# Layer 0 of a two-layer net: feature parts stored once and repeated by the loads, and other places for three streams in a step

## The chip, the cores and the metric

The kernel runs on one core of one Trainium2 chip. Its time is the device time of one execution in microseconds, median over runs.

## What is computed

64 batches of 128 rows of 128 features go through two layers, each of an attention and a mixture of experts, each added to its input through a tanh gate. The change touches the attention of layer 0, a cross-attention whose scores are taken on exponential features:

```python
def _feature_map(x, fm_w, fm_b):
    z = jnp.einsum('nshd,ed->nshe', x, fm_w) + fm_b
    return jnp.concatenate([jnp.exp(z), jnp.exp(-z)], axis=-1)

v, k, q = (_feature_map(x, fm_w, fm_b) for x in (v, k, q))     # 16 heads of 8 -> 16 features
scores = jnp.einsum('nqhd,nkhd->nhqk', q, k) / jnp.sqrt(128.)
attn = jax.nn.softmax(scores, axis=-1)
out = jnp.einsum('nhql,nlhd->nqhd', attn, v)
...
x = x + jnp.tanh(g_xattn[0]) * (out @ fc_w.T + fc_b)           # q from layernorm(x), k and v from the context (77 rows)
x = x + jnp.tanh(g_ffn[0]) * ffn0(layernorm(x))                # 8 experts, 1 to 6 of them by a router
x = x + jnp.tanh(g_xattn[1]) * attention1(layernorm(x), context)   # relative positions
x = x + jnp.tanh(g_ffn[1]) * ffn1(layernorm(x))                # 8 experts, two per row
```

## The kernel before

**Units and steps.** In layer 0 the 64 batches make 16 groups of four for the experts and 32 units of two for the attention (NU = 2; UT = 256 columns of queries, UK = 154 of context). Step k works on several units at once, each in another stage, as Python generators ("streams"): `l0_project(k-3)`, `l0_weighted(k-2)`, `l0_maxima(k-1)` and `l0_features(k)`; in every second step the router of a group; and beside them the `tape` of the experts, some 16 parts in a step. Two steps are a pair: an even step with the router, an odd one without. Layer 1 has its own steps after these.

**What sets the order.** `weave` calls the streams' parts by time within the step. `PLAN` gives each stream (start, end, priority, behind): its parts are spread evenly between the shares start and end of a step; the priority is handed to the scheduler, which orders the instructions of each engine; `behind` = n makes the PE instructions of the stream stand after the (n+1)th last part of the experts traced so far. Each engine then takes its instructions in this order. All DMAs of layer 0 go out on SP's queue (`nc.sync`), in order.

**The attention of a unit, in four streams.**

- `l0_features` (L290): loads x and the context, layer norm, transposes (pt, L304 and L306), one matmul (pz, L311), four exps on ACT into f, the values' transposes (pv, L327). As f32 products are taken from bf16 parts, `split3` (L132) cuts f into three bf16 parts f3: cast on DVE, subtract on POOL, cast, subtract. The product of two such numbers takes six pairs of parts, and these six stand as 96 rows (6 pairs × 16 features of a head) of qst for the queries and kst for the context. To get from 128 partitions (features × heads) to these rows, the parts go through DRAM: `stack_out` stores dq and dk with each part repeated as the pairs want it (six stores, L144 and L146, 1,230 KB), and four loads (L340, L342) bring 48 rows at a time to qst and kst, in rows of 512 and 308 bytes.
- `l0_maxima` (L346): scores S (L355) of all heads, maxima mx over the context (L358), a transpose pn (L363), and the negated maxima in three bf16 parts, n3 (L366 to L369), sent as three rows of 8 KB into qst, rows 96 to 98 (L371). kst has ones there, so that the second product takes the maximum away by itself.
- `l0_weighted` (L373): ST (L396), the scores again, transposed and without their maxima; exp to P (L399); products with the values, AV (L385), which also give the denominators; a copy to av (L388) and a store to od in DRAM (L408, 512 KB). Then `normalize` (L428): denominators den from od (L435), o in two loads (L439), a reciprocal on DVE (L440), dr to DRAM sixteen times repeated (L442, 256 KB), rr back (L445), o times rr on POOL (L446).
- `l0_project` (L411): the output product pf (L420) and x1.

The experts (`l0_ffn`) make three-fold f32 products on PE by a helper (L165 to L167) with the tiles pg, pu and py; between them ACT and DVE compute t (L516 to L518), ACT hh (L523) and POOL hl (L524).

Of the kernel before, what the change touches and what calls it, by code (L numbers as in the profile page):

```python
# [10 lines left out]
F32 = mybir.dt.float32  # L11
F32R = mybir.dt.float32r
BF16 = mybir.dt.bfloat16
AF = mybir.ActivationFunctionType
# [6 lines left out]
KL = 77  # L21
NH = 16
# [6 lines left out]
NU = 2  # L29
UT = NU * S  # L30
UK = NU * KL
# [10 lines left out]
def weave(tc, streams, marks=None):  # L42
# [27 lines left out]
PARTS0, PARTS1 = 33, 24  # L70

PLAN = dict(
    out=(0,0.2,2000,0),
    wei=(0, 0.7, 0, 6),
    max=(0.05, 0.8, 1000, None),
    fea=(0.2, 0.6, 500, None),
    out1=(0.1, 0.25, 600, None),
    att1=(0.25, 1.1, 0, 8),
    rel1=(0.32, 0.88, 0, 3),
# [25 lines left out]
class Net:  # L105
# [26 lines left out]
    def split3(self, f, out3):  # L132
# [3 lines left out]
        nc.gpsimd.tensor_tensor(f, f, out3[:, 0], ALU.subtract)  # L136
        nc.vector.tensor_copy(out3[:, 1], f)
        nc.gpsimd.tensor_tensor(out3[:, 2], f, out3[:, 1], ALU.subtract)  # L138

    def stack_out(self, dq, dk, f3, nq):  # L140

        nc = self.nc
        for n, c, p in ((0, 3, 0), (3, 2, 1), (5, 1, 2)):
            nc.sync.dma_start(out=dq[n : n + c].rearrange("i p t -> p i t"),  # L144
                              in_=f3[:, p, :nq].unsqueeze(1).to_broadcast([128, c, nq]))
            nc.sync.dma_start(out=dk[n : n + c].rearrange("i p t -> p i t"), in_=f3[:, :c, nq:])  # L146

    def stack_q(self, dq, f3, nq):
        for n, c, p in ((0, 3, 0), (3, 2, 1), (5, 1, 2)):
# [140 lines left out]
    def l0_features(self, u, st):  # L290
        nc, i, tc = self.nc, self.i, self.tc
        a, pm, dp = self.ap, self.pmisc, self.dp
        b0 = u * NU
        kst, (vf, va) = self.kst[u % 3], self.va[u % 3]
        xg = self.f0.tile([128, NU, 128], F32, tag="xg", bufs=4, name="xg")
        nc.sync.dma_start(out=xg, in_=i["x"][b0 : b0 + NU].rearrange("b p d -> p b d"))
        cg = a.tile([KL, NU, 128], F32, tag="cg", bufs=2, name="cg")
        nc.sync.dma_start(out=cg, in_=i["ctx_1024"][b0 : b0 + NU].rearrange("b p d -> p b d"))
        xn = self.layernorm(xg, NU, a, "a")
        nc.gpsimd.tensor_tensor(xg, xg, self.fcb.unsqueeze(1).to_broadcast([128, NU, 128]), ALU.add)  # L300
        NT = UT + UK
        pt = pm.tile([128, 512], F32, tag="misc", name="pt")
        for b in range(NU):
            nc.tensor.transpose(pt[:, b * S : (b + 1) * S], xn[:, b, :], self.ident)  # L304
        for b in range(NU):
            nc.tensor.transpose(pt[:, UT + b * KL : UT + (b + 1) * KL], cg[:, b, :], self.ident[:KL, :KL])  # L306
        xT = a.tile([128, NT], F32, tag="xT", bufs=1, name="xT")
        nc.scalar.copy(xT, pt[:, :NT])
        yield
        pz = pm.tile([128, 512], F32, tag="misc", name="pz")  # L310
        nc.tensor.matmul(pz[:, :NT], lhsT=self.fmW, rhs=xT, start=True, stop=True)  # L311

        f = a.tile([128, 2 * NT], F32, tag="feat", bufs=1, name="feat")
        for n, sign in ((0, 1.0), (1, -1.0)):
            nc.scalar.activation(f[:, n * UT : (n + 1) * UT], pz[:, :UT], AF.Exp, bias=self.fmb[:, n : n + 1], scale=sign)
            nc.scalar.activation(f[:, 2 * UT + n * UK : 2 * UT + (n + 1) * UK], pz[:, UT:NT], AF.Exp,
                                 bias=self.fmb[:, n : n + 1], scale=sign)
        yield
        if u < 3:
            with tc.issue_after(self.ln_last.ins):  # L320
                nc.vector.memset(kst[96:99], 1.0)
            nc.gpsimd.memset(va[:, :, :, 16:17], 1.0)

        for b in range(NU):
            pv = pm.tile([128, 512], F32, tag="misc", name="pv")
            for s in range(2):
                nc.tensor.transpose(pv[:KL, s * 128 : (s + 1) * 128],  # L327
                                    f[:, 2 * UT + s * UK + b * KL : 2 * UT + s * UK + (b + 1) * KL], self.ident)
            nc.scalar.copy(va[:, b, :, 0:16],
                                  pv[:KL, :256].rearrange("p (c h) -> p h c", h=NH))  # L330
        f3 = a.tile([128, 3, 2 * NT], BF16, tag="f3", bufs=1, name="f3")
        yield
        self.split3(f, f3)
        yield
        dq = dp.tile([6, 128, 2 * UT], BF16, tag="dq", name="dq")
        dk = dp.tile([6, 128, 2 * UK], BF16, tag="dk", name="dk")
        self.stack_out(dq, dk, f3, 2 * UT)
        qst = a.tile([99, NH, UT], BF16, tag="qst", bufs=3, name="qst")
        for n in range(2):
            nc.sync.dma_start(out=qst[48 * n : 48 * n + 48],  # L340
                              in_=dq[:, :, n * UT : (n + 1) * UT].rearrange("i (e h) t -> (i e) h t", h=NH))
            self.last_dma = nc.sync.dma_start(out=kst[48 * n : 48 * n + 48],  # L342
                              in_=dk[:, :, n * UK : (n + 1) * UK].rearrange("i (e h) t -> (i e) h t", h=NH))
        st[u] = dict(xg=xg, qst=qst, kst=kst, va=vf, spare=[Spare(self.pGU, self.gub)] * 4 if u < 2 else [])

    def l0_maxima(self, s):  # L346
# [26 lines left out]
    def l0_weighted(self, s):  # L373

        nc, a = self.nc, self.ap
        ps_t, qst, kst, va = self.pST, s["qst"], s["kst"], s["va"]
        av = a.tile([128, 4, NU, 128], F32, tag="av", bufs=1, name="av")
        vp = self.avp
        banks = itertools.cycle([ps_t] + s["spare"][2:])

        def weigh(b, hg, p):
            for j in range(4):

                n = (b * NH + 4 * j + hg) * 17
                nc.tensor.matmul(vp[32 * j : 32 * j + 32, hg, :], lhsT=va[:, n : n + 32],  # L385
                                 rhs=p[:, j, :], start=True, stop=True, tile_position=(0, 32 * j))
            if hg == 3:
                nc.scalar.copy(av[:, :, b, :], vp)  # L388

        last = None  # L390
        for b in range(NU):
            for hg in range(4):
                st = next(banks).tile([128, 4, 128], F32, tag="ST", name="ST")
                for j in range(4):
                    h = 4 * j + hg
                    nc.tensor.matmul(st[:KL, j, :], lhsT=kst[:, h, b * KL : (b + 1) * KL],  # L396
                                     rhs=qst[:, h, b * S : (b + 1) * S], start=True, stop=True)
                p = a.tile([KL, 4, 128], F32, tag="P", bufs=3, name="P")
                nc.scalar.activation(p, st[:KL], AF.Exp, scale=1.0 / math.sqrt(128.0))  # L399
                if last:  # L400
                    weigh(*last)
                last = (b, hg, p)
                yield
        weigh(*last)
        yield
        T = NU * S
        od = self.dp.tile([4, 32, 4, T], F32, tag="od16", name="od")
        nc.sync.dma_start(out=od.rearrange("j r g t -> (j r) g t"), in_=av.rearrange("p g b q -> p g (b q)"))  # L408
        s["o"] = self.normalize(od, 16, NU)

    def l0_project(self, u, s, x1s):  # L411
        nc, pm = self.nc, self.pmisc
# [12 lines left out]
            x1s[u // 2] = self.x1n  # L425
        yield

    def normalize(self, od, nd, n):  # L428


        nc, a, dp = self.nc, self.ap, self.dp
        nch = nd * NH // 128
        T = n * S
        den = a.tile([NH * n, 128], F32, tag="den", bufs=1, name="den")
        nc.sync.dma_start(out=den, in_=od[:, nd].rearrange("j g (b q) -> j (g b) q", b=n))  # L435
        o = self.f0.tile([128, nch, T], F32, tag="o", bufs=2, name="o")
        ny = 4 // nch
        for y in range(ny):
            nc.sync.dma_start(out=o[y::ny], in_=od[:, :nd, y * nch : (y + 1) * nch].rearrange("j d c t -> d j (c t)"))  # L439
        nc.vector.reciprocal(den, den)  # L440
        dr = dp.tile([nd, NH * n, 128], F32, tag=f"dr{nd}_{n}", name="dr")
        nc.sync.dma_start(out=dr.rearrange("d p q -> p d q"),  # L442
                          in_=den.unsqueeze(1).to_broadcast([NH * n, nd, 128]))
        rr = a.tile([128, nch, T], F32, tag="rr", bufs=1, name="rr")
        nc.sync.dma_start(out=rr, in_=dr.rearrange("d (x c b) q -> (d x) c (b q)", c=nch, b=n))  # L445
        nc.gpsimd.tensor_tensor(o, o, rr, ALU.mult)  # L446
        return o

# [814 lines left out]
```

## Time and profile before

| | |
|---|---|
| three runs | 2716.01, 2718.08 and 2725.01 us; median 2718.08 |
| the profiled execution | 2721.63 us, its span 2719.9 us |
| mean granted TensorE clock | 0.94 |
| layer 0 | about the first 1345 us of the span |
| DMA | 282.16 MB, 468,652 packets |
| PE idle, 0 to 120 us, S L355 for kst<-dk | 20.6 us, 3 times, the longest 11.5 |
| PE idle, 120 to 1330 us, S L355 for kst<-dk | 28.0 us, 16 times |

The page gives the busy time of each engine: PE is TensorE's matmuls, PEld its loads of weights, DVE, ACT and POOL the vector, scalar and GpSimd engines, SP the engine that issues the DMAs. It cuts the span into 40 slices with the busy share in tenths, where PEclk is the clock that TensorE was granted, in tenths of full speed. The chain that ended last is followed back from the end, from each instruction to what released it. A row of the timeline has the start and length in us, the engine, the line and operation with its tiles (out<-in), and in brackets the idle time ahead of it and what ended that. "L355" is line 355 of the kernel.

### The profile page before, as it was taken

How to read it: one execution, taken by the hardware profiler on the slowest of the kernel's cores; microseconds unless marked ns; L12 is line 12 of the kernel's file. 1: busy time of each engine (PE TensorE's matmuls, PEld its weight loads, DVE VectorE, ACT ScalarE, POOL GpSimd, SP SyncE). 2: the span in 40 equal slices, each digit the busy share in tenths (PEclk: the TensorE clock that was granted, in tenths of full speed). 3: DMA queues.
4: the chain of work that ended last, by engine and by line, in shares of the span. 5: the costliest groups of instructions: out<-in, count | busy, mean ns of one | idle time of the engine just before them, and what ended most of it. 6: DMA issues, size and time to landing. Idle time of an engine off the chain costs nothing.

```text
span 2719.9 us, 60927 instructions
## 1 busy us (share of the span) xinstructions
PE 2409.3 (89%) x23574; PEld 1655.9 (61%) x23574; DVE 1996.1 (73%) x4165; ACT 1563.2 (57%) x3030; POOL 1551.5 (57%) x1508
## 2 busy tenths in 40 slices
PE   3688989999989899999897798998999998999996
PEld 2466666666666666666565565666666666666654
DVE  3368788888888888887785466776677676766676
ACT  2455555656555556555454356666666666666665
POOL 4455465555565555554566355665666666656556
PEclk9989899999999999999997689999999999999999
DMA  6744355354454443453235655545555655655400
GB/s 140 172 107 93 78 114 117 93 107 104 83 122 106 94 111 91 100 120 73 57 80 130 137 115 112 119 110 107 107 112 109 121 127 116 126 111 109 95 16 8
DMA packets 468652, 282.16 MB, mean 104 GB/s; under 512 B 231030, under 2 KB 446974, under 8 KB 468267
## 3 DMA queue, kind: packets, MB, share of 16 engines
q1 hardware_dynamic: 440715, 237.89, 43.4%
q10 hardware_dynamic: 27648, 40.38, 4.3%
q8 instruction: 185, 3.03, 0.5%
q14 instruction: 104, 0.85, 0.1%
HBM read 143.00 MB, written 134.40 MB: 102 GB/s over the span
## 4 chain that ended last, share of the span: by engine, by line
PE 49%; DMA 16%; DVE 13%; POOL 9%; issue 7%; ACT 3%; SPq 3%; POOLq 0%; ACTq 0%; DVEq 0%
DMA kst<-dk 5%; PE ST L837 4%; PE py L165 3%; PE py L166 3%; PE py L167 3%; PE AV L845 3%; DMA dk<-f 2%; PE AV L385 2%; POOL hl L1001 2%; PE S L780 2%; PE pu L165 2%; PE pg L165 2%; PE pz L165 2%; PE S L885 2%; POOL f L138 2%
## 5 line engine op out<-in xcount | busy, mean ns | idle before, releaser
L524 POOL TENSOR_TENSOR hl<-t,hh 128x512 fp32r<-128x512 f32 x336 | 441.8, 1317 | 352.3 <-ACT hh L523 348.2
L1001 POOL TENSOR_TENSOR hl<-t,hh 128x512 fp32r<-128x512 f32 x256 | 347.0, 1371 | 148.0 <-ACT hh L1000 145.3
L829 POOL TENSOR_TENSOR sc<-sc,mx 128x308 f32<-128x308 f32 x256 | 190.3, 747 | 229.4 <-DVE mx L828 94.8
L523 ACT CAST hh<-t 128x512 fp32r<-128x512 f32 x336 | 207.2, 617 | 162.5 <-PE py L167 68.8
L516 ACT ACTIVATE t<-pg 128x512 f32<-128x512 f32 x336 | 200.9, 598 | 158.3 <-PE pg L167 114.2
L517 DVE SCALAR_TENSOR_TENSOR t<-t,pg 128x512 f32<-128x512 f32 x336 | 227.7, 678 | 74.6 <-ACT t L516 74.0
L838 ACT ACTIVATE rel<-ST 77x512 f32<-77x512 f32 x256 | 157.7, 616 | 170.4 <-PE ST L837 166.7
L518 DVE TENSOR_TENSOR t<-t,pu 128x512 f32<-128x512 f32 x336 | 227.3, 677 | 15.1 <-PE pu L167 6.7
L623 DVE TENSOR_TENSOR ys<-sb,py 128x512 f32<-128x512 f32 x224 | 152.0, 679 | 79.2 <-PE py L167 78.3
L827 DVE TENSOR_TENSOR sc<-S,rq 128x308 f32<-128x308 f32 x256 | 120.2, 472 | 120.6 <-PE ST L837 50.3
L614 ACT COPY sb<-pb 128x512 f32<-128x512 f32 x256 | 150.5, 588 | 97.4 <-PE pb L609 94.2
L837 PE MATMUL ST<-ident,sc 128*128 128x128 f32 (+1 forms) x1024 | 173.9, 296 | 35.1 <-POOL sc L829 33.0
L1000 ACT CAST hh<-t 128x512 fp32r<-128x512 f32 x256 | 155.5, 622 | 83.6 <-PE py L167 75.0
L993 ACT ACTIVATE t<-pz 128x512 f32<-128x512 f32 x256 | 151.9, 600 | 69.9 <-POOL hl L1001 64.1
L399 ACT ACTIVATE P<-ST 77x512 f32<-77x512 f32 x256 | 151.0, 591 | 57.9 <-PE ST L396 55.1
L165 PE MATMUL py<-hh,wd_h 128*128 128x512 f32 x336 | 156.9, 467 | 18.5 <-ACT sb L614 11.9
L165 PE MATMUL pg<-xh,wg_h 128*128 128x512 f32 x336 | 159.9, 476 | 11.5 <-DVE t L518 10.5
L358 DVE TENSOR_REDUCE mx<-S 128x5 f32<-128x385 f32 (+1 forms) x192 | 110.4, 577 | 78.2 <-PE S L355 76.6
L837 PEld LDWEIGHTS ST<-ident,sc 128*128 128x128 f32 (+1 forms) x1024 | 126.4, 152 | 66.6 <-POOL sc L829 42.0
L165 PE MATMUL pu<-xh,wu_h 128*128 128x512 f32 x336 | 159.9, 476 | 5.0 <-DVE t L517 4.5
L166 PE MATMUL py<-hl,wd_h 128*128 128x512 f32 x336 | 148.6, 442 | 2.3 <-POOL hl L524 2.3
L995 DVE TENSOR_TENSOR t<-t 128x512 f32<-128x512 f32 x128 | 106.6, 833 | 50.9 <-ACT t L993 50.8
(247 smaller groups left out, 6627.4 us busy)
## 6 DMA issues: line engine op xcount, KB each, us to landing
rq<-ra SPq DMA_DIRECT2D x256, 154.0 KB
qst<-dq SPq DMA_DIRECT2D x96, 384.0 KB
ra<-sg ACTq DMA_DIRECT2D x128, 192.5 KB
kst<-dk SPq DMA_DIRECT2D x96, 231.0 KB
dq<-f SPq DMA_DIRECT2D x47, 384.0 KB
od<-av SPq DMA_DIRECT2D x32, 512.0 KB
ra<-sg ACTq DMA_DIRECT2D x64, 231.0 KB
dq<-f SPq DMA_DIRECT2D x47, 256.0 KB
```

The lines of the kernel that those rows point to most:

```text
L165: nc.tensor.matmul(ps, lhsT=wh, rhs=xh, start=start, stop=False)
L166: nc.tensor.matmul(ps, lhsT=wh, rhs=xl, start=False, stop=False)
L516: nc.scalar.activation(t, pg, AF.Tanh, scale=0.5)
L517: nc.vector.scalar_tensor_tensor(t, t, 1.0, pg, ALU.add, ALU.mult)
L518: nc.vector.tensor_tensor(t, t, pu, ALU.mult)
L523: nc.scalar.copy(hh, t)
L524: nc.gpsimd.tensor_tensor(hl, t, hh.bitcast(F32), ALU.subtract)
L829: nc.gpsimd.tensor_tensor(sc, sc, m.unsqueeze(2).to_broadcast([128, 4, KL]), ALU.subtract)
L837: nc.tensor.transpose(st[:r, j, :], sc.rearrange("q j k -> q (j k)")[:, j * KL : j * KL + r], self.ident)
L838: nc.scalar.activation(relg[:KL, hg, b], st[:KL].rearrange("k j (q e) -> k j q e", e=2), AF.Exp, scale=1.0 / math.sqrt(HD))
L1000: nc.scalar.copy(hh, t)
L1001: nc.gpsimd.tensor_tensor(hl, t, hh.bitcast(F32), ALU.subtract)
```

## The change

Three things change in layer 0.

First, `l0_features` writes f in another layout (positive exps of queries and context together, then the negative ones), so that two exps do instead of four, and stores each of the three parts once: d01 with parts 0 and 1, d2 with part 2 (615 KB in all). The repeats that the six pairs want are made by the loads, six in place of four, which read the same part of DRAM for several groups of rows: the same number of rows, of the same sizes, now at a pitch of 820 bytes for both. Two of the six need d2.

Second, `normalize` takes den straight from av in SBUF in place of od in DRAM, stores dr once (16 KB) and repeats it in the load of rr.

Third, in `PLAN` the shares of features, weighted sums and output change, and the weighted sums stand behind the experts' part two further back.

```diff
 PLAN = dict(
-    out=(0,0.2,2000,0),
-    wei=(0, 0.7, 0, 6),
+    out=(0, 0.3, 2000, 0),
+    wei=(0.15, 0.85, 0, 8),
     max=(0.05, 0.8, 1000, None),
-    fea=(0.2, 0.6, 500, None),
+    fea=(0.05, 0.45, 500, None),
...
-    def stack_out(self, dq, dk, f3, nq):
-
-        nc = self.nc
-        for n, c, p in ((0, 3, 0), (3, 2, 1), (5, 1, 2)):
-            nc.sync.dma_start(out=dq[n : n + c].rearrange("i p t -> p i t"),
-                              in_=f3[:, p, :nq].unsqueeze(1).to_broadcast([128, c, nq]))
-            nc.sync.dma_start(out=dk[n : n + c].rearrange("i p t -> p i t"), in_=f3[:, :c, nq:])
...
         for n, sign in ((0, 1.0), (1, -1.0)):
-            nc.scalar.activation(f[:, n * UT : (n + 1) * UT], pz[:, :UT], AF.Exp, bias=self.fmb[:, n : n + 1], scale=sign)
-            nc.scalar.activation(f[:, 2 * UT + n * UK : 2 * UT + (n + 1) * UK], pz[:, UT:NT], AF.Exp,
-                                 bias=self.fmb[:, n : n + 1], scale=sign)
+            nc.scalar.activation(f[:, n * NT : (n + 1) * NT], pz[:, :NT], AF.Exp, bias=self.fmb[:, n : n + 1], scale=sign)
...
-                                    f[:, 2 * UT + s * UK + b * KL : 2 * UT + s * UK + (b + 1) * KL], self.ident)
+                                    f[:, s * NT + UT + b * KL : s * NT + UT + (b + 1) * KL], self.ident)
...
-        dq = dp.tile([6, 128, 2 * UT], BF16, tag="dq", name="dq")
-        dk = dp.tile([6, 128, 2 * UK], BF16, tag="dk", name="dk")
-        self.stack_out(dq, dk, f3, 2 * UT)
+
+        d01 = dp.tile([2, 256, NT], BF16, tag="d01", name="d01")
+        d2 = dp.tile([1, 256, NT], BF16, tag="d2", name="d2")
+        for d, p0, p1 in ((d01, 0, 2), (d2, 2, 3)):
+            nc.sync.dma_start(out=d.rearrange("i (n p) t -> p (i n) t", n=2),
+                              in_=f3[:, p0:p1].rearrange("p i (n t) -> p (i n) t", n=2))
+
         qst = a.tile([99, NH, UT], BF16, tag="qst", bufs=3, name="qst")
-        for n in range(2):
-            nc.sync.dma_start(out=qst[48 * n : 48 * n + 48],
-                              in_=dq[:, :, n * UT : (n + 1) * UT].rearrange("i (e h) t -> (i e) h t", h=NH))
-            self.last_dma = nc.sync.dma_start(out=kst[48 * n : 48 * n + 48],
-                              in_=dk[:, :, n * UK : (n + 1) * UK].rearrange("i (e h) t -> (i e) h t", h=NH))
+        q, k = slice(0, UT), slice(UT, NT)
+        for to, row, n, src in ((qst, 0, 3, d01[:1, :, q]), (kst, 16, 2, d01[:, :, k]), (qst, 48, 2, d01[1:, :, q]),
+                                (kst, 80, 1, d01[:1, :, k]), (qst, 80, 1, d2[:, :, q]), (kst, 0, 1, d2[:, :, k])):
+            src = src.rearrange("i p t -> (i p) t")
+            rows = n * src.shape[0] // 16
+            if n > 1:
+                src = src.unsqueeze(0).to_broadcast([n, *src.shape])
+            self.last_dma = nc.sync.dma_start(out=to[row : row + rows], in_=src)
...
-        s["o"] = self.normalize(od, 16, NU)
+        s["o"] = self.normalize(av, od, 16, NU)
...
-        nc.sync.dma_start(out=den, in_=od[:, nd].rearrange("j g (b q) -> j (g b) q", b=n))
+        nc.sync.dma_start(out=den, in_=av[nd::32].rearrange("j g b q -> j (g b) q"))
...
-        dr = dp.tile([nd, NH * n, 128], F32, tag=f"dr{nd}_{n}", name="dr")
-        nc.sync.dma_start(out=dr.rearrange("d p q -> p d q"),
-                          in_=den.unsqueeze(1).to_broadcast([NH * n, nd, 128]))
+        dr = dp.tile([NH * n, 128], F32, tag=f"dr{nd}_{n}", name="dr")
+        nc.sync.dma_start(out=dr, in_=den)
         rr = a.tile([128, nch, T], F32, tag="rr", bufs=1, name="rr")
-        nc.sync.dma_start(out=rr, in_=dr.rearrange("d (x c b) q -> (d x) c (b q)", c=nch, b=n))
+        nc.sync.dma_start(out=rr, in_=dr.rearrange("p q -> (p q)").unsqueeze(0).to_broadcast([nd, NH * n * 128]))
```

More of the change, by code (lines that the diff above doesn't have):

```diff
@@ L426, in l0_project, with normalize @@
         yield
-    def normalize(self, od, nd, n):
+    def normalize(self, av, od, nd, n):
         nc, a, dp = self.nc, self.ap, self.dp
```

## The prediction

> **What bounds the kernel now.** I read the page first: the slices of section 2, then the chain.
>
> ```profile
> PE 2409.3 (89%) x23574; PEld 1655.9 (61%) x23574; DVE 1996.1 (73%) x4165; ACT 1563.2 (57%) x3030; POOL 1551.5 (57%) x1508
> PE   3688989999989899999897798998999998999996
> PEclk9989899999999999999997689999999999999999
> PE 49%; DMA 16%; DVE 13%; POOL 9%; issue 7%; ACT 3%; SPq 3%; POOLq 0%; ACTq 0%; DVEq 0%
> ```
>
> PE is the bound, but in the first half (layer 0, up to about 1345 us; the change touches nothing behind it) its slices are not full, and 16% of the chain is DMA. Next, the waits of PE between 120 and 1330 us (line waited for, total us, times, longest):
>
> ```profile
> PE S L355 <- DMA kst<-dk: 28.0, 16, 3.0
> PE ST L396 <- DMA qst<-n: 25.0, 17, 2.4
> PE pg L165 <- DVE t L518: 10.5, 14, 1.6
> ```
>
> Two waits lead, and both have a DMA at their end. They come in turn: a pair of units takes 82.5 us; in its even step the scores S wait for the last load (mean 2.25 us over 13 pairs), in its odd step the weighted scores ST wait for the third row of maxima (mean 1.8; 2.05 in the pair shown below). Third, windows of 2 us around one such ST wait (busy us of PE, PEld, DVE, ACT, POOL, then granted clock, DMA share, GB/s):
>
> ```profile
> 844.00:846.00 2.00, 0.41 (x2) 0.11 (x1) 2.00 (x1) 0.75 (x2) 2.00 (x2) 1.00 0.54 167
> 846.00:848.00 2.00, 1.28 (x6) 0.96 (x6) 2.00 (x4) 1.11 (x2) 0.72 (x2) 0.59 0.15 28
> 848.00:850.00 2.00, 2.00 (x6) 1.54 (x5) 1.97 (x3) 0.00 (x0) 0.66 (x1) 0.50 0.88 176
> 850.00:852.00 2.00, 2.00 (x6) 1.58 (x5) 0.92 (x2) 1.07 (x2) 1.04 (x1) 0.50 1.27 129
> 852.00:854.00 2.00, 2.00 (x16) 1.26 (x16) 1.90 (x3) 1.25 (x3) 1.51 (x2) 0.71 1.23 171
> ```
>
> The reader is to see the second price: after the idle stretch the clock is 0.50 for nearly 7 us. It does so after nearly every wait of 1.6 us or more (about 30 between 120 and 1345 us; 0.50 for 3.4 or 6.8 us, mean 4.5) and after none of 1.06 us or less. At half clock PE does half the work, so a drop costs about 2.2 us, as much as the wait itself.
>
> Last, the SP queue of an even step, with the S it feeds:
>
> ```profile
> 869.81 0.36 SPq L144 DMA_DIRECT2D dq<-f  x1
> 870.22 3.23 SPq L146 DMA_DIRECT2D dk<-f  x2
> 876.16 0.55 SPq L342 DMA_DIRECT2D kst<-dk  x1
> 876.80 0.58 SPq L408 DMA_DIRECT2D od<-av  x1
> 881.67 0.78 SPq L435 DMA_DIRECT2D den<-od  x1
> ```
>
> ```profile
> 887.63 0.55 PE L355 MATMUL S<-kst,qst 96*128 96x77 bf16 x6 [2.46 <-DMA kst<-dk]
> ```
>
> The first load is issued only at 876.16, when the stores have landed (3.1 us after their last issue), and the loads with od's 512 KB among them need 11.5 us to S. SP moves data in the order of issue: rows of n were seen to move only behind load rows issued before them.
>
> **The change part by part.** By the instruction orders PE and DVE and POOL run as many instructions as before; SP loses 64 rows, ACT 64 exps (0.3 us a unit, off the path).
>
> *Even step, S.* The parts one and two (d01) can be stored when the second cast is done, near 870.2, where dk's second store is issued today; the third part goes last and the loads that need it too. So 870.2 + 3.1 = 873.4 for the first load, 2.7 us earlier. The bytes loaded (1,230 KB) and their row sizes (512 and 308 B) stay; so does od among them. All is landed at 887.6 − 2.7 = 884.9. PE now arrives at 887.63 − 2.46 = 885.2 and by its new order 0.9 us earlier (22.0 us of PE work between pz and S before, 21.1 after): 884.3. The wait becomes 0.6 to 0.7 instead of 2.25, −1.5 for a pair; over 13 pairs −20. A wait of 0.7 was followed by no drop: −2.2 × 13 = −29. That the features' share starts at 0.05 moves S no further from its features, as these distances show; in the odd step they fall from 18.9 to 14.7, and odd S has waited 0.35 on average, so this may cost it up to 1 us (inside the bounds of the odd step below).
>
> *Rows at another pitch.* The loads of q read 512 B rows at 820 B instead of 1,024. No such row is in the trace; the nearest are the 308 B rows of k at 616 B pitch and the aligned 512 B rows:
>
> ```profile
> 932.00:933.50 1.50, 1.50 (x5) 1.22 (x4) 1.50 (x2) 0.33 (x1) 0.41 (x1) 0.50 0.83 163
> 934.00:937.50 3.50, 3.50 (x23) 2.59 (x22) 2.17 (x3) 2.21 (x4) 2.50 (x2) 0.84 1.27 120
> ```
>
> 163 GB/s for the first, 120 for the second: the crooked pitch was no slower, so I take nothing. The even step's 1,230 KB in 8.1 us are 155 GB/s; were the 768 KB of q to move at 163 or 120, a unit would gain 0.3 or lose 1.5 us. The Trainium skill ("DMA: Bandwidth & Descriptors", "How a descriptor splits into AXI transactions") speaks against the change: a read that does not start on a 256 B boundary fetches further beats; a 512 B row would need up to 24 instead of 16, an estimate of 1.5 times for 768 of the 1,230 KB, or 2.5 us a unit; with it S waits over 3 us, its drops stay, and the sum ends near 2750.
>
> *Stores.* 616 KB instead of 1,230 KB are written for each unit. No engine waits for the second half as such, so this counts only in the earlier landing, bounded by 0 and −0.7.
>
> *Even step, new waits.* The denominators go straight from SBUF, and the reciprocal stands earlier on DVE, ahead of the maxima's remainder and of the experts' t. Its load is queued behind loads and od, landing about 21.5 us after pz; DVE stops there, behind it the t products, behind these pg and pu: I take +0.9 (none to +2). The n rows stand behind dr and rr on SP; today the last is issued 25.3 us after pz (861.44) and lands 2.9 later, at 28.2; two more issues ahead of it make 29. PE's work between pz and ST is 25.3, with the 0.7 and 0.9 above and some 1.4 of small waits 28.3: +0.7 (0 to +2). Together +1.6 × 13 = +21. Both are short enough to drop no clock.
>
> *Odd step, ST.* Today the third n row is issued 12.4 us after pz on average and ST runs at 15.3, waiting about 2.0. After: pn stands 2.1 earlier, so the row is issued at 10.4, but three loads, 692 KB, are now ahead of it in the queue. 1,230 KB took 8.1 us, so 692 take 4.6; with 1.3 from issue to the first packet it lands at 16.3, and PE (0.7 us more work between pz and ST) arrives at 14.0: a wait of 2.3, +0.3, with its drop as now: +4 (−0.5 to +2.5 a pair: −6 to +32).
>
> *Start-up.* S of the first unit waits 11.47 us. Its loads go out 3.6 earlier, unit 1's about 6, the expert weights 4.5; od no longer stands ahead of den (2.27 us), and dr writes 16 KB instead of 256. The first expert's pg at 115.95 hangs on unit 1's chain, which takes over after the weights: −6 (0 to −12). End of layer 0: −1.
>
> Sum: −20 − 29 + 21 + 4 − 6 − 1 = −31 against the profiled execution's 2721.63 (span 2719.9 and 1.7 around it), so 2690.6; from the median 2718.08 it is 2687. I say 2690.
>
> On the clock the trace and a page differ. The Trainium skill ("TensorE: Matmul & The Clock Gate", "Why this matters for your kernels") asks only for no gaps above some 3 us; by it waits of 2 to 3 us are free of clock cost, and the sum is −2, about 2719. The 0.50 after a wait of 2.05 us in the windows above decides for the row.
>
> **The rivals.** *R1, slower.* The repeated loads stand ahead of the third n row in the odd step. The point is its landing: if it must wait for more than the 692 KB ahead of it, up to all 1,230 (8.1 us), ST waits 1.3 to 3.7 more, mean 2.5, and the drop lasts 6.8 instead of 3.4 us (+1.7): +4.2 a pair. With the even step's net of −2.15 that is +2.05 × 13 = +27, −7 for the start: 2741, or 2738 from the median. For it: SP's order and a wait that already is 2 us. Against: load rates of 120 to 163 GB/s need only 4.3 to 5.9 us for 692 KB. It decides when the row lands over 2 us later than I reckon.
>
> *R2, the gain is handed on.* S no longer waits, but the den and ST waits that follow in the same step grow past 1.6 us and the clock drops there instead: with ten of the thirteen drops back, −20 − 29 + 21 + 22 − 7 = −13: about 2709 from the profiled execution. For it: den is queued behind 1.2 MB. Against: PE's queue has expert products from other parts between.
>
> *R3, the change doesn't do what it says:* shares that begin at 0.05 and 0.15 and a lag of 8 might put more work between feature and score. The distances above say no (21.1 and 14.7), so it is part of R2.
>
> **How the numbers follow.** My forecast, 0.58: 2650 to 2708 (low: −20 − 29 − 6 − 12 − 1 with no new waits, from the median; high: half of the drops stay and the new waits come in full). R2 0.17, R1 0.25 (2735 to 2745 and beyond). The range of 2648 to 2736, its low end a little under the lowest sum, holds nearly all of the first two and the lower part of R1, leaving out some 0.17. This kernel's measurement can tell about 0.3%, 8.2 us, from no change: the forecast and a little of R2 lie below 2709.9 (0.61); the rest of R2 is within (0.14); R1 is above (0.25).
>
> **What would show it.** Right: S L355 waiting for its loads under 10 us in all between 120 and 1330 us; the clock at 0.50 some 13 times less often; ST L396 still about 25 us; a pair at 80 to 80.5 us; the first pg some 6 us earlier. R1: ST L396 over 50 us with mean waits near 4.5. R2: few S waits, but as many drops, after pg, pu or ST. Wrong altogether: S waiting as long as now (the rows at 820 B are slow, or d01 does not go out at the second cast), or layer 1 moving by more than 3 us.

## The result and the profile after

The changed kernel takes 3417.62 us (median of four runs, 3408.5 to 3424.15) against 2721.55 before: a ratio of 1.255 (95% interval 1.251 to 1.260). The forecast was 2690. The page of the changed kernel (engines' busy time, the slices of PE, the granted clock):

```profile
PE 2452.0 (72%) x23574; PEld 1681.6 (49%) x23574; DVE 1971.2 (58%) x4165; ACT 1555.5 (46%) x2966; POOL 1553.9 (45%) x1508
PE   1356575575576575575575589788999999999997
PEclk9978788787788787788787799789999999999998
```

PE, DVE and POOL run as many instructions as before, and PE's busy time hardly grew (43 us); the slices of layer 0 are half empty. Layer 1 did not move: from the last output product of layer 0 to PE's last instruction it takes 1364.9 us, 1365.3 before. All 698 us are in layer 0. PE's waits over the whole span (line waited for, total us, times, longest):

```profile
PE S L352 <- DMA kst<-d: 479.3, 32, 31.6
PE ST L393 <- DMA qst<-n: 268.3, 18, 20.2
```

The two waits that led before still lead, at 748 us in place of 77. The timeline of SP's queue shows one unit (start, us, line, tiles), and PE's timeline the S that it feeds:

```profile
828.89 2.20 SPq L329 DMA_DIRECT2D d<-f  x2
832.67 0.76 SPq L340 DMA_DIRECT2D qst<-d  x1
833.49 8.07 SPq L340 DMA_DIRECT2D kst<-d  x1
841.62 11.60 SPq L340 DMA_DIRECT2D qst<-d  x1
853.26 5.71 SPq L340 DMA_DIRECT2D kst<-d  x1
859.07 0.54 SPq L405 DMA_DIRECT2D od<-av  x1
```

```profile
866.12 0.55 PE L352 MATMUL S<-kst,qst 96*128 96x77 bf16 x6 [23.60 <-DMA kst<-d]
```

An issue takes 0.6 us where the queue is free. Here the second, third and fourth load are held for 8, 12 and 6 us each: the loads ahead of them are still moving, as the windows below show. From the first load to S are 33.5 us; it was 11.5. How slowly they move stands in three windows of the changed kernel (busy us of PE, PEld, DVE, ACT, POOL, then clock, DMA share, GB/s): the load of 48 query rows (three copies), of 64 context rows (two copies), of 32 query rows (two copies):

```profile
836.00:842.00 6.00, 6.00 (x30) 4.38 (x30) 4.00 (x10) 3.26 (x8) 3.47 (x3) 1.00 0.23 47
846.00:851.00 5.00, 0.00 (x0) 0.00 (x0) 0.00 (x0) 0.00 (x0) 0.00 (x0) 0.50 0.15 35
856.00:859.00 3.00, 0.00 (x0) 0.00 (x0) 0.00 (x0) 0.00 (x0) 0.00 (x0) 0.50 0.15 39
```

47, 35 and 39 GB/s, where the loads of before had 120 to 163. The DMA share is the clue: 0.23 and 0.15 of sixteen engines are 3.7 and 2.4, in the proportion of three copies to two. (The share adds up the times of packets, which overlap, so that it can pass 1; it gives the proportion and does not count the engines.) In packets it is 91, 113 and 77 rows a us; the three loads have 768, 1024 and 512 rows, so 8.4 + 9.1 + 6.6 = 24.1 us a unit. A pair of units takes 128.0 us in place of 83.6 (means over twelve pairs), 22.2 more a unit, and 32 units make 710 us, near the 698 measured.

### The profile page after: what moved, and what is told of

Read it like the earlier page. It is cut to its first block, busy times and chain, and to the rows that moved or that the text cites. A ratio compares the mean times of both kernels' runs of the same rounds, so it can differ in the third digit from the quotient of the medians.

```text
span 3418.1 us, 60728 instructions
## 1 busy us (share of the span) xinstructions
PE 2452.0 (72%) x23574; PEld 1681.6 (49%) x23574; DVE 1971.2 (58%) x4165; ACT 1555.5 (46%) x2966; POOL 1553.9 (45%) x1508
## 5 line engine op out<-in xcount | busy, mean ns | idle before, releaser
L352 PE MATMUL S<-kst,qst 96*128 96x77 bf16 x1024 | 76.8, 218 | 481.0 <-DMA kst<-d 479.3
L352 PEld LDWEIGHTS <-qst 96*128 96x128 bf16 x1024 | 54.4, 108 | 523.7 <-issue 294.5
L393 PE MATMUL ST<-qst,kst 99*77 99x128 bf16 x1024 | 109.8, 236 | 269.3 <-DMA qst<-n 268.3
L393 PEld LDWEIGHTS <-kst 99*77 99x77 bf16 x1024 | 93.3, 128 | 315.0 <-issue 234.7
L437 DVE RECIPROCAL den<-den 32x128 f32<-32x128 f32 x32 | 30.0, 937 | 308.0 <-DMA den<-av 307.9
L157 PE MATMUL pu<-xh,wu_h 128*128 128x512 f32 x336 | 171.1, 509 | 15.7 <-DVE t L513 15.6
```

Of the source, the lines that this page charges most:

```text
L157: nc.tensor.matmul(ps, lhsT=wh, rhs=xh, start=start, stop=False)
```

## The experiments

Three theories were set against each other: (1) a load whose leading dimension counts 3 or 2 copies runs on 3 or 2 DMA engines; (2) repeated rows, or rows 820 bytes apart, are read slowly; (3) the new order in the step does it. All runs, in the order they were made, with the ratio to the kernel before in the same chip session (its median was 2714 to 2722):

| run | us | ratio (95%) |
|---|---|---|
| split | 2774.88 | 1.019 (1.016–1.023) |
| plan_norm | 2763.02 | 1.015 (1.012–1.019) |
| lead2 | 3019.56 | 1.110 (1.106–1.113) |
| wide | 2725.99 | 1.002 (1.000–1.004) |
| plan_only | 2732.38 | 1.007 (1.004–1.009) |
| norm_only | 2772.78 | 1.023 (1.018–1.028) |
| split_oldplan | 2746.03 | 1.012 (1.008–1.016) |
| wide_oldplan | 2719.55 | 1.002 (1.000–1.004) |
| norm_late | 2778.54 | 1.023 (1.020–1.026) |
| wide_late | 2727.91 | 1.003 (1.002–1.005) |
| wide_feat_only | 2717.74 | 1.000 (0.997–1.002) |
| feat_only | 3489.73 | one run |
| norm_fix | 2742.99 | 1.010 (1.006–1.013) |
| split_feat_only | 2790.03 | 1.026 (1.022–1.029) |
| split_nact | 2787.76 | 1.024 (1.020–1.029) |
| wide_nact | 2711.43 | 0.998 (0.996–1.000) |
| wide_split | 2695.99 | 0.993 (0.991–0.995) |

### What the 700 us are

**split**: the repeats as single loads.

```diff
-            rows = n * src.shape[0] // 16
-            if n > 1:
-                src = src.unsqueeze(0).to_broadcast([n, *src.shape])
-            self.last_dma = nc.sync.dma_start(out=to[row : row + rows], in_=src)
+            rows = src.shape[0] // 16
+            for j in range(n):
+                self.last_dma = nc.sync.dma_start(out=to[row + j * rows : row + (j + 1) * rows], in_=src)
```

> The changed kernel with each repeated load written as single loads one after the other (ten loads instead of six; same bytes, same rows, same pitch of 820 bytes, same parts of DRAM read as often). Theory 1, a load whose leading dimension counts 3 or 2 copies is moved by 3 or 2 of the 16 DMA engines: every load now has a leading dimension of 16, S no longer waits, and the time falls from 3417 to 2690 (2650 to 2740), as the prediction reckoned. Theory 2, repeated rows or rows at a pitch of 820 bytes are read slowly: the rows and repeats are the same, so 3300 to 3450. Theory 3, the new places in the step and the reciprocal ahead of the experts on DVE do it: 3300 to 3450.

2775: 643 of the 696 us are gone with the bytes, the rows and the pitch unchanged. Theories 2 and 3 fall as explanations of the bulk. S still waits for its loads, but 18.7 us between 120 and 1330 us (28.0 before). In a window of split in which nearly every packet is a context row of the single loads (756 rows of 308 bytes, 420 a us), the rate is back:

```profile
875.20:877.00 1.80, 0.89 (x7) 0.74 (x7) 0.35 (x1) 0.47 (x1) 0.00 (x0) 0.92 1.37 130
```

But 2775 lies above the range of theory 1 and is not 2690; that is the second question below.

**plan_norm**: the kernel before with the new PLAN and the new `normalize`, no new features.

> The kernel before with the new PLAN and the new normalize, but its own features (six stores, four loads). Theories 1 and 2 (the loads of the features): the time stays near the 2720 of before, 2660 to 2760, and S waits for its loads no longer than 3 us anywhere after the start. Theory 3 (order): 3200 to 3450.

2763, 3 us above the range of theory 1 and far from theory 3; S waits up to 4.4 us, where 3 was the bound. So the order is not the 700, yet it is not free.

**lead2**: split with the two parts of a row side by side in DRAM, so that two loads of 32 context rows have a leading dimension of 2 without a repeat.

```diff
-        d01 = dp.tile([2, 256, NT], BF16, tag="d01", name="d01")
-        d2 = dp.tile([1, 256, NT], BF16, tag="d2", name="d2")
+        d01 = dp.tile([256, 2, NT], BF16, tag="d01", name="d01")
+        d2 = dp.tile([256, 1, NT], BF16, tag="d2", name="d2")
...
+            rows = 32 if len(src.shape) == 3 else 16
+            if rows == 32:
+                src = src.rearrange("p i t -> i p t")
```

> As split, but the two parts of a context row stand side by side in DRAM, so that the two loads of 32 rows of kst have a leading dimension of 2 without any repeat (512 rows of 308 bytes each; three stores instead of two). Theory 1: these two loads run on two engines at the 113 packets per us that the changed kernel showed, 4.5 us each instead of about 1.2, 6.6 us a unit; with 3 to 5.5 of them as idle PE in each of 32 units, 100 to 180 us above split. Theory 2 (repeats): the same as split, within 30 us.

3020, 245 above split and more than reckoned: 7.7 us a unit, where the two loads were to take 6.6 longer. One of them fills this window of lead2, with DMA share 0.15 as for the two copies of the changed kernel:

```profile
878.00:881.00 3.00, 1.44 (x7) 1.06 (x8) 2.65 (x9) 0.86 (x3) 0.26 (x1) 1.00 0.15 36
```

It is the count of the leading dimension and not the repeat.

**wide**: the other side of the same question. Repeats inside a load, but as the second dimension behind 16 features; for this, queries and context of a part stand by themselves, so that a row is one piece.

```diff
+            if src is dks:
+                src = src.rearrange("i (e h) t -> e i (h t)", h=NH)
+            else:
+                src = src.rearrange("(e h) t -> e (h t)", h=NH)
+                if n > 1:
+                    src = src.unsqueeze(1).to_broadcast([16, n, src.shape[1]])
+            self.last_dma = nc.sync.dma_start(out=to[row : row + 16 * n].rearrange("r h t -> r (h t)"), in_=src)
```

> As the change, but queries and context of each part stand in DRAM by themselves, so that a row of qst or kst is one piece of 8192 or 4928 bytes, and the loads repeat a part with the 16 features as the leading dimension and the copies as the second (eight loads; six stores of half the bytes). Theory 1: repeats inside a load cost nothing when the leading dimension is 16: 2640 to 2700, at or under split. Theory 2 (repeats inside a load are slow): well above split, over 2900.

2726: repeats inside a load are not slow. The hoped-for gain did not come.

**feat_only**: the new features alone.

> The new features and their six loads alone, with the PLAN and the normalize of before. Theory 1 (loads on 3 and 2 engines are the loss by themselves, and the rest adds some 40 us): 3330 to 3420; S and ST waiting over 600 us together.

3490 in one run, above the range: the slow loads do it by themselves. S and ST wait 551.5 us together, under the 600 expected, and pu another 215.0 for t on DVE. That the new PLAN and `normalize` take back some 70 us while the loads are slow rests on this one run.

Theory 1 stands. The Trainium skill says it outright ("DMA: Bandwidth & Descriptors", "Rules for kernel authors" and "Why a DMA increments its semaphore by 16 and not by 1"): a DMA runs on the largest number of engines, up to 16, that divides the slowest dimension (of a size other than 1) of both sides, so a leading broadcast of c copies holds it to at most c. The traces agree: DMA shares in the proportion of 3 to 2 for counts of 3 and 2 (the views do not name the engine of a packet), and full rates for 16.

### Why it is not 2690 with fast loads

**plan_only, norm_only, split_oldplan, wide_oldplan**: which of PLAN and `normalize` costs the 41 us of plan_norm.

> The kernel before with the new PLAN alone. The kernel with the new PLAN and the new normalize stood 41 us above before. Theory A, the moved shares cost it (weighted sums and features of a step meet other work): +30 to +50 us, 2750 to 2770. Theory B, the new normalize costs it: within 10 us of before.

> The kernel before with the new normalize alone (den straight from SBUF, dr stored once, repeated by the load of rr). Theory A: -10 to +5 us against before. Theory B (the reciprocal stands earlier on DVE and stops the experts there): +30 to +50 us.

> The split kernel (features stored once, ten single loads, new normalize) with the PLAN of before. Theory A: 40 to 55 us under split, 2715 to 2740. Theory B: like split, 2765 to 2785.

> The wide kernel (rows of 8192 and 4928 bytes, repeats inside loads with a leading dimension of 16, new normalize) with the PLAN of before. Theory A: 2665 to 2700, faster than before by over 0.7%. Theory B: like wide, 2715 to 2735.

PLAN alone costs 18 us and `normalize` alone 59; together 41, so they do not add up. Theory B is nearer, but plan_only lies in neither range and norm_only above B's; and B's reason does not show: in norm_only DVE waits 0.2 us in all for the denominators (5.1 before). split_oldplan is 29 under split (21, each against the kernel before of its own session), between the two forecasts; wide_oldplan lies level with wide. In norm_only, S waits 68.4 us for its loads between 120 and 1330 us (28.0 before):

```profile
PE S L355 <- DMA kst<-dk: 68.4, 24, 4.7
```

POOL's timeline of a unit in norm_only and before (the two subtractions of the feature parts are `feat<-feat,f` and `f<-feat,f`):

```profile
956.00 1.75 POOL L136 TENSOR_TENSOR feat<-feat,f 128x820 f32<-128x820 f32 x1
957.71 1.74 POOL L523 TENSOR_TENSOR hl<-t,hh 128x512 fp32r<-128x512 f32 x1
960.65 1.29 POOL L445 TENSOR_TENSOR o<-o,rr 128x512 f32<-128x512 f32 x1 [1.19 <-DMA rr<-dr]
...
962.28 1.74 POOL L138 TENSOR_TENSOR f<-feat,f 128x820 bf16<-128x820 f32 x1
```

```profile
919.46 1.76 POOL L136 TENSOR_TENSOR feat<-feat,f 128x820 f32<-128x820 f32 x1 [1.76 <-PE pv L327]
921.76 1.47 POOL L524 TENSOR_TENSOR hl<-t,hh 128x512 fp32r<-128x512 f32 x1 [0.54 <-ACT hh L523]
923.19 2.21 POOL L138 TENSOR_TENSOR f<-feat,f 128x820 bf16<-128x820 f32 x1
```

With the shorter chain of den, the scheduler puts o times rr between the two subtractions (in 9 of 24 units; the expectation of norm_fix says ten), where it waits for rr. The odd units' first load goes out 17.8 us after pz instead of 15.1. Three runs were to test whether this is what costs the time.

**norm_late**: the multiplication written at the start of `l0_project`.

> The kernel with the new normalize alone (2773 us, where POOL stops 3 us in every second step for rr ahead of o times rr, and S waits 68 us for its loads), with one line moved: o times rr is written down at the start of the unit's output stream, a step later, so that POOL takes it after the feature parts and hl that were queued behind it. Theory B1 (the multiplication stands too early in POOL's order and stops the feature parts behind it): POOL's wait for rr under 10 us in all, S waiting near 30 us, time 2705 to 2730. Rival B2 (the den and rr transfers themselves are in the way of the loads): POOL's wait gone, but S still over 55 us and 2755 or more.

POOL's wait for rr stayed (47.8 us; 49.7 in norm_only), and the multiplication still stands between the subtractions in 9 of 24 units: the moved line did not move the instruction, perhaps because of the output stream's priority. So the run tells nothing. **wide_late** tells nothing on this either: in wide_oldplan, which it starts from, the multiplication stands there in none of 24 units, and POOL's wait for rr went from 36.2 to 43.4 us.

> The wide loads with the PLAN of before and the new normalize (2720 us, POOL stopping 1.4 us in each unit for rr), with the same line moved. Theory B1: 2685 to 2710, faster than before by 0.3 to 1%. Rival B2: no change against 2720.

**norm_fix**: the order forced.

```diff
+        mult = nc.gpsimd.tensor_tensor(o, o, rr, ALU.mult)
+        self.tc.add_manual_dep(mult.ins, self.parts_done.ins.name, mybir.DependencyInfo(
+            mybir.DependencyClass.NoSync, mybir.DependencyReason.DATA), reason="order")
```

> The kernel before with the new normalize, and o times rr held behind the third feature part of the same step in POOL's order (an order only, no wait for data). In norm_only it stood between the feature parts in 10 of 24 units and stopped POOL for rr there. Theory B1: the parts come out as early as before, S waits about 30 us for its loads, and the time is 2705 to 2735. Rival B2 (the den and rr transfers are in the way): S still over 55 us, 2755 or more.

2743, between the two, with single runs from 2724 to 2765: about half of the 59 us went. The multiplication now stands between the subtractions in none of 24 units, and the first load of the odd units is issued at 15.8 instead of 17.8. But in the profiled run, which took 2761.61 us, S waits as long as in norm_only, as rival B2 said, and POOL still waits for rr, now behind the feature parts:

```profile
PE S L356 <- DMA kst<-dk: 69.7, 28, 3.5
POOL o L446 <- DMA rr<-dr: 54.0, 11, 8.4
```

So the multiplication among the feature parts may be a part of the cost of `normalize`; the trace does not show it, and the rest stays open.

**wide_feat_only, split_feat_only**: the features alone, in both forms of fast loads.

> The wide loads alone, with the PLAN and the normalize of before. If the early multiplication on POOL is what keeps the wide kernels from gaining (B1): 2680 to 2710. If the wide loads gain nothing by themselves, because another wait (ST for its n rows) takes over: 2710 to 2725.

> Features stored once and fetched by ten single loads, with the PLAN and the normalize of before. If the residue of split (2775) comes from normalize and PLAN: 2690 to 2725. If it comes from the features themselves (two more loads that wait for the third part, rows at 820 bytes): 2740 or more.

Level with before, and 75 us slower. The reason given for the second range of wide_feat_only does not show: ST's wait for the n rows did not take over (21.6 us, 25.0 before), S itself still waits 29.1 us (28.0 before). And most of split's residue comes with the features themselves, not with PLAN and `normalize`.

**split_nact, wide_nact**: the n rows on ACT's queue (`nc.scalar.dma_start` in `l0_maxima`).

> Split with the three n rows issued from ACT's queue instead of SP's. If ST's 37 us of waiting come from loads that stand ahead of the n rows on SP: ST's waits for n fall under 15 us and the time by 25 to 50 us, to 2725 to 2750. If they come from the n rows being made late: ST's waits stay and the time is within 15 us of split.

> The wide loads with the PLAN and normalize of before (2718), with the n rows on ACT's queue. Same question: 2685 to 2705 if the rows stand behind loads on SP, 2710 to 2730 if not.

In split, ST's waits for n fell from 36.9 to 12.0 us as the first branch said, and the time rose by 13: S waited 31.0 and 13.5 us for kst and qst instead of 18.7 for kst, and pu 37.4 for t instead of 29.5. What ST no longer waited, S and pu did. In wide it is 6 us under wide_feat_only, within what can be told, and 2711 lies in the range of the second branch.

**wide_split**: the number of loads against the form of their rows.

```diff
+        for to, row, src in ((qst, 0, dqs[0]), (qst, 16, dqs[0]), (qst, 32, dqs[0]), (kst, 16, dks[0]), (kst, 48, dks[0]),
+                             (kst, 80, dks[0]), (qst, 48, dqs[1]), (qst, 64, dqs[1]), (kst, 32, dks[1]), (kst, 64, dks[1]),
+                             (qst, 80, dqs[2]), (kst, 0, dk2[0])):
+            self.last_dma = nc.sync.dma_start(out=to[row : row + 16].rearrange("r h t -> r (h t)"),
+                                              in_=src.rearrange("(e h) t -> e (h t)", h=NH))
```

> The wide features alone (PLAN and normalize of before), with every repeat as a load of its own: twelve loads of 16 rows, each row one piece of 8192 or 4928 bytes. If the number of loads on SP's queue is what costs split_feat_only its 75 us: 2770 or more. If it is the short rows (512 and 308 bytes, 820 apart): 2705 to 2735, as wide_feat_only with its eight loads.

2696 with twelve loads, faster than both kernels and than every range given: the number of loads on SP is not what costs split_feat_only its 75 us. What differs besides is that rows are whole, and that every store and load waits for one part only: the first load is issued 4.2 us (even units) and 6.6 us (odd) after pz instead of 14.2 and 15.1, and S runs at 21.6 and 23.7 instead of 25.5 and 26.2. These two were not told apart. The nearest run, wide_feat_only, has both of them, the same six stores and whole rows; it differs from wide_split in its eight loads alone. Its first load goes out at 4.8 and 7.2 us and its S runs at 20.3 and 22.1, earlier still, yet it takes 22 us longer. So neither of the two alone explains 2696, and what the single loads bring there is open. PE's waits of wide_split between 120 and 1330 us:

```profile
PE ST L393 <- DMA qst<-n: 22.3, 21, 3.0
PE S L352 <- DMA kst<-dk: 11.3, 10, 1.5
```

S's wait for its last loads falls from 28.0 to 11.3 us; ST's stays at 22.3.

## Why the prediction was wrong

**The step that failed** is in "Even step, S": "The bytes loaded (1,230 KB) and their row sizes (512 and 308 B) stay", from which the loads kept their 11.5 us to S. Bytes and rows did stay; the number of DMA engines that move them did not: the loads moved at 35 to 47 GB/s instead of 120 to 163, and from the first load to S it became 33.5 us. The term had no line of its own. It was worth 22 us a unit, 44 a pair, where the sum had −1.5 a pair. The section on pitch asked whether such rows are slow, and looked for it in the rows alone; the shape of the new loads, whose first dimension is the copies, was in the diff. The sign "S waiting as long as now" came, but for neither of the two reasons that stood beside it.

**The first load**: reckoned 2.7 us earlier. Measured from pz, it goes out at 12.9 instead of 14.2 in even units and at 10.9 instead of 15.1 in odd ones. Right in kind, half of it in even units.

**The pitch**: taken as nothing. In split, whose loads run on 16 engines, a packet of 512 bytes takes 52 ns on average, 53 before (all packets of that size between 120 us and the end of layer 0, more than half of them query rows): in this mean the further beats that the Trainium skill ("DMA: Bandwidth & Descriptors", "How a descriptor splits into AXI transactions") gives for rows off a 256 B boundary do not show. A packet of 308 bytes, all of them context rows, takes 45 ns where it took 29 at the pitch of 616. A unit has 1,536 of them, 96 to an engine: 1.5 us that the prediction did not have. But the pitch alone does not make them slow: in the changed kernel the same rows at the same pitch of 820 bytes take 24 ns. What makes them slower in split, where the loads follow each other on 16 engines, was not tested.

**The new waits**: reckoned +21 us for the reciprocal on DVE and the n rows. The reciprocal's wait was small where the loads were fast (12.1 us in all in split, 0.2 in norm_only). `normalize` alone costs 59 all the same, by a way that is not known; the place of o times rr on POOL had no term at all.

**The moved shares**: taken as free; alone they cost 18 us (4 to 9 thousandths).

**The clock**: a drop was priced at 2.2 us. The stretch of twelve pairs from unit 6 to unit 30, before and in wide_feat_only (span and PE's busy time lead, the clock is third from the end):

```profile
188.60:1192.30 1003.70, 919.69 (x6222) 642.86 (x6220) 848.86 (x1614) 578.05 (x1161) 564.91 (x504) 0.94 0.46 102
```

```profile
171.80:1185.90 1014.10, 908.59 (x6247) 619.34 (x6258) 823.06 (x1609) 581.87 (x1120) 575.41 (x506) 0.98 0.33 86
```

The clock was at half for 118.4 us before and for 41.0 in wide_feat_only, and PE's busy time is only 11.1 us less. For the 16 drops that went, that is 0.7 us each, a third of the price; by this comparison the term of −29 would have been about −9. It is not the price of a drop alone, as the two kernels order their work differently: before, a 128x512 f32 matmul starts 427 ns after the last one at a clock of 0.50 and 234 at 1.00 (medians), so that a busy PE does do little more than half the work at half clock. Where the rest of the gain went is open. The idle time rose meanwhile, from 84.0 to 105.5 us, most of it in waits of the experts for DVE (pg and pu for t: 10.9 us before, 27.2 after); their waits for ACT fell.

The condition of a drop did not carry over either. Of PE's idle stretches of 1.6 us or more between 120 and 1330 us, 25 of 27 were followed by a clock of 0.50 before, but 8 of 15 in wide_feat_only, where the longest without a drop is 2.53 us.

**Start-up**: reckoned −6. plan_norm has its first pg at 110.1 instead of 115.9, so PLAN and `normalize` bring it; with slow loads it came at 195.1. **Layer 1** was right.

**The rivals**: R1 named the loads ahead of the n rows as the danger. ST does wait 268 us for these rows, but as a consequence: R1's price went by load rates of 120 to 163 GB/s, and they were 35 to 47. R3 named the start shares; with PLAN alone (plan_only) they cost 18 us, so the 700 are not theirs. None of the three had the mechanism.

What stays open: why the single loads of short rows cost 75 us as a whole (longer packets make some 1.5 us of 2.4 a unit, and not all of that need reach the end), why twelve single loads of whole rows gain 22 us over eight, what the cost of `normalize` comes from, and why PLAN and `normalize` together cost less than `normalize` alone. Each edit gave the scheduler another order on every engine, and these orders were not held fixed.

## What to carry to other kernels

Before a load's time is taken over from another load of the same bytes, its access pattern is to be read from the slowest dimension on both sides: here a count of 2 or 3 there took the rate from some 130 GB/s to 35 or 47. Copies belong behind a dimension of 16, or into loads of their own. Storing less brought nothing by itself (split_feat_only is 75 us slower than before, wide_feat_only level with it); the one gain came with whole rows in single loads (2696). And a shorter chain can cost time: norm_only, whose denominators come earlier, lost 59 us. There the scheduler had moved the chain's last instruction ahead of work that others wait for; look at that engine's order too, though how much of the loss this makes was not shown.

## What the runs showed of the hardware

A load with a leading dimension of 2 or 3 also holds up its queue: while such loads moved, SP's next issues took 8.07, 11.60 and 5.71 us instead of 0.6, and what stood behind them waited, the n rows above all (ST waits 268 us for them). With a leading dimension of 2, rows of 308 bytes moved at 113 a us where the dimension was copies (846 to 851 us of the changed kernel) and 116 where it was parts (878 to 881 of lead2); single loads of such rows moved 420 a us in split's window. And an idle PE of 1.6 us or more was followed by a clock of 0.50 nearly always in the kernel before (25 of 27, the longest 3.0 us), but in about half of the cases in wide_feat_only (8 of 15, the longest 3.7).
